# A selective-scan hybrid kernel: ScalarE's share for other stages follows a timetable of VectorE's units, and a turn gets two rooms for its column sums

## The chip, the cores and the metric

The kernel runs on one core of a Trainium2 chip. The metric is device time in microseconds (us). Three runs of the kernel before took 6051.08, 6039.0 and 6030.13 us; the median is 6039.0 us.

## The reference, cut to what matters

Four layers run on x of shape 4 x 96 x 64 x 64, image by image. Layer 0 is a selective scan over four directions k; layers 1 to 3 (an inverted-bottleneck convolution, a Fourier mixing layer with a small quantised feed-forward, a linear attention with another) need only matmuls and elementwise work. The scan is what must be seen:

```python
xs = jnp.stack([xf, xt, jnp.flip(xf, -1), jnp.flip(xt, -1)], axis=1)   # rows, columns, both reversed
def step(hst, inp):
    ut, dt_, bt, ct = inp
    dA = jnp.exp(dt_[..., None] * A[None])
    hst = hst * dA + (dt_ * ut)[..., None] * bt[:, :, None, :]
    y = jnp.einsum('bkdn,bkn->bkd', hst, ct)
    return (hst, y)
...
y = y0 + y1 + y2 + y3      # y1 and y3 come back from column order to row order
```

There are 192 channels d, 16 states n, 4096 positions, 4 directions and 4 images.

## The kernel before, in words

**Units and slots.** A unit of the scan is a tile of 128 rows (32 channels x 4 states) and 1024 positions. There are 4 images x 4 directions x 4 pieces of 1024 x 24 tiles = 1536 units. `scans` (L1234) is a Python loop over slots, one unit a slot, which writes the order of the instructions of every engine's queue by hand. A unit takes these steps:

- POOL multiplies the input by B (`inputs`, L1278, the instruction is L1280), two slots ahead, into one of 8 buffers `scan_w`.
- ScalarE makes the decay exp(delta A) (`decays`, L1282, L1287), one slot ahead, into one of two pairs of PSUM banks `ps_da`. Just ahead of it stands `keep` (L1309, L1315), which copies the last state of the unit before.
- VectorE runs the scan (`states`, L1297, L1303). The multiplication by C (`product`, L1318) follows on VectorE at once, or on POOL two slots later. `share` (L1289) chooses, so that a planned lead of the two engines over each other stays small; it uses planned times of 2.35 us for a scan and 1.2 or 2.37 us for a product.
- TensorE sums the 4 states of a channel into `ps_y` (`sums`, L1331, L1341), two units at a time, three slots later. ScalarE copies a finished `ps_y` to `yt` (`sums_out`, L1350, L1355), and SyncE stores it.

With two pairs of banks, the decay of slot s+1 can start when VectorE has left unit s-1, and it has to be done before VectorE has left unit s. Whatever stands between two decays in ScalarE's queue uses up that time.

**The other stages** stand in the same queues, beside the scan. `plan` (L1225) lists them as stages, each a set of generators that yield (engine, planned us) before an instruction, or `wait(n)` for n slots: fronts (input convolution and scan inputs of the next image), weights, turns, conv, spectral, layer_2, layer_3. At the end of each slot `advance` (L1467) issues steps of the current stage while its engine still has room (`fits`, L1454: at least half of the step's planned time). A TensorE result is used by ScalarE in the same slot only while little TensorE work has been planned in it. The room is refilled at the end of each slot by fixed amounts with a cap (`SHARE`, L59; L1404): 2.4 us up to 2.8 for ScalarE, 3.0 up to 3.2 for TensorE, 1.5 up to 2.0 for VectorE.

**A turn** (`turn`, L646) brings the sums of the two column directions back to row order and adds the row direction and the skip term. It works on three thirds of 64 channels. A third loads the two column directions into the tile `ya`, 1 MB each (L657), waits 10 slots, goes through 8 chunks (small loads L666 and L667, matmuls L672 and L674, an eviction L678, a store), and waits 2 slots. The turns of images 0 and 1 are stages of their own; those of images 2 and 3 run beside layer_3 of the image before. `big` (L198) has two buffers in all while the scans run.

**After the last unit** (image 3's convolution, spectral and last layers) no scan remains to run beside.

Of the kernel before, what the change touches and what calls it, by code (L numbers as in the profile page):

```python
# [46 lines left out]
SCAN_US, PRODUCT_US = 2.35, (1.2, 2.37)  # L47
# [8 lines left out]
WORK = {"weights": 47.0, "turn": 79.2, "front": 417.0, "conv": 447.0,  # L56
        "spectral": 111.2, "layer_2": 231.0, "product": 1.2, "layer_3": 153.6, "layer_3_turn": 232.8}
RATE = 6.0
SHARE = {"pe": (3.0, 3.2), "act": (2.4, 2.8), "dve": (1.5, 2.0)}  # L59
NQ, NG, NPAIR = 4, HID // 32, H // 2  # L60


# [35 lines left out]
def hybrid_kernel(ctx: ExitStack, tc: tile.TileContext, a: dict):  # L98


    pe, ac, dv = ((lambda us, banks=0, ind=False, e=e: (e, us, banks, ind)) for e in ("pe", "act", "dve"))
    wait = lambda n: ("wait", n, 0, False)
    nc = tc.nc
    mm = nc.tensor.matmul
    act = nc.scalar.activation
# [3 lines left out]
    pool = lambda name, bufs=1, **kw: ctx.enter_context(tc.tile_pool(name=name, bufs=bufs, **kw))  # L109
# [10 lines left out]
    def turns(of):  # L120
        of.append(of.pop(0))
        return of[-1]
# [33 lines left out]
    def const(name, rows=slice(0, 128)):  # L156
        return cst[rows, CS[name]]
# [40 lines left out]
    def big(name):  # L198
        if last_room and turns(thirds) == "last":
            return last_room[0].tile([128, 6144], F32, name=name, tag="big", bufs=1)  # L200
        return bp.tile([128, 6144], F32, name=name, tag="big", bufs=2)
# [4 lines left out]
    spare = []  # L206
# [44 lines left out]
    def split(t):  # L251
        return t.rearrange("p (a b) -> p a b", a=RPC)
# [393 lines left out]
    def turn(b):  # L646


        im = b % 2
        early = b == B - 1  # L650
        while scanned[b] < (2 if early else 3) * NCH:
            yield wait(1)
        t = big("ya")
        for r in (2, 0, 1) if early else (0, 1, 2):
            lo = 64 * r
            for at, k in ((0, 1), (64, 3)):
                load(t[at : at + 64, :L].rearrange("p (c l) -> p c l", c=NCH),  # L657
                     d_y[k][im][:, lo : lo + 64, :].rearrange("c p l -> p c l"))

            rows = not (early and r == 2)  # L660
            held = slice(0 if rows else 64, 128)

            def fetch(c):
                u = t[:, L + c % 4 * CH : L + c % 4 * CH + CH]
                if rows:
                    load(u[:64], d_y[0][im][c, lo : lo + 64])  # L666
                load(u[64:], d_skip[b][c, lo : lo + 64])  # L667
                return u

            def added(p, of):  # L670
                c, u = of
                mm(split(p[:64]), lhsT=const("two")[:, :64],  # L672
                   rhs=t[:, :L].rearrange("p (w h) -> p h w", h=H)[:, c * RPC : (c + 1) * RPC, :], start=True, stop=False)
                mm(p[:64], lhsT=skips[held, r], rhs=u[held], start=False, stop=True)  # L674

            def stored(p, of):
                s = tmp("yrow")[:64]
                nc.scalar.copy(s, p[:64])  # L678
                later(d_yt[im][of[0]][lo : lo + 64], s)

            chunks = ahead(1, fetch, range(NCH))

            ready = (lambda n: scanned[b] >= 2 * NCH + min(n + 2, NCH)) if early and rows else (lambda n: True)
            yield wait(10)
            yield from in_turn(chunks, pe(2.7, 1), added, ac(0.6), stored, ready=ready)
            yield wait(2)

    def scan_outputs(b, done):

# [544 lines left out]
    def scans(stages):  # L1234
# [13 lines left out]
        units = []  # L1248
# [33 lines left out]
        def decays(x, last):  # L1282
            if last is not None:
                keep(last)
            av = (x["step"]["k"] * NI + x["i"]) * NJ + x["j"]
            x["da"] = decay_banks()
            act(x["da"], x["step"]["d"][x["i"]], AF.Exp, scale=aneg[:, av : av + 1])  # L1287

        def share(x):  # L1289

            on_vector, on_pool = PRODUCT_US
            lead = ahead_by[0] + SCAN_US - on_pool
            x["pool"] = abs(lead - on_pool) < abs(lead + on_vector)
            lead += -on_pool if x["pool"] else on_vector
            ahead_by[0] = max(-AHEAD, min(lead, AHEAD))

        def states(x):  # L1297
            step, u = x["step"], x["u"]
            share(x)
            order = slice(None, None, -1) if step["k"] >= 2 else slice(None)  # L1300
            x["h"] = x["w"] if x["pool"] else x["da"]
            start = 0.0 if step["n"] == 0 else steps[x["number"] - 1]["last"][:, u : u + 1]
            nc.vector.tensor_tensor_scan(  # L1303
                x["h"][:, order], x["da"][:, order], x["w"][:, order], start, ALU.mult, ALU.add
            )
            if not x["pool"]:
                product(x, nc.vector)
# [23 lines left out]
        def sums(group):  # L1331
            step, first, last = group[0]["step"], group[0]["j"] == 0, group[0]["j"] == NJ - 1
            if first:
                step["y"] = bank("y")
            y = step["y"]

            made = None
            for m in (1, 0):
                for e in (1, 0):
                    q = 2 * e + m  # L1340
                    done = mm(y[32 * q : 32 * q + 32], lhsT=const("stack"), rhs=group[m]["w"][:, e * CH : e * CH + CH],  # L1341
                              start=first, stop=last)
                    if made is None:
                        made = group[0]["made"]
                        tc.add_manual_dep(done.ins, made.ins.name, mybir.DependencyInfo(
                            mybir.DependencyClass.Sync, mybir.DependencyReason.DATA), reason="sums")
            if last:
                summed.append((group, y))

        def sums_out():  # L1350
            while summed:
                group, y = summed.pop(0)
                step = group[0]["step"]
                yt = sp.tile([128, CH], F32, name="yt", bufs=1)
                nc.scalar.copy(yt, y)  # L1355
                which = group[0]["pass"]
                for e in (0, 1):
                    to = d_y[step["k"]][step["b"] % 2][2 * step["c"] + e]
                    later(to[64 * which : 64 * which + 64], yt[64 * e : 64 * e + 64],
                          (lambda b=step["b"]: through(b)) if which == len(PASSES) - 1 and e == 1 else None)  # L1360
# [9 lines left out]
        inputs(units[0])  # L1370
        inputs(units[1])
        decays(units[0], None)
        for slot in range(len(units) + 6):
            clock[0] = slot
            x = units[slot] if slot < len(units) else None
            if x is not None:
                if x["u"] == 0:


                    last = len(units) - NST * PC  # L1380
                    if slot < last:
                        rate = max(RATE, sum(s.work for s in stages if s not in behind) / (last - slot))
                    else:
                        rate = sum(s.work for s in stages) / (len(units) - slot)
                for name, i in OWN.get(x["u"], ()):
                    fetch(x["step"], name, i)
                if x["number"] + 1 < len(steps) and x["u"] in LOADS:
                    if x["u"] == 14:
                        need(steps[x["number"] + 1])
                    for name, i in LOADS[x["u"]]:  # L1390
                        fetch(steps[x["number"] + 1], name, i)
            flush()
            if slot + 1 < len(units):
                decays(units[slot + 1], units[slot - 1] if slot > 0 else None)
            sums_out()
            if slot + 2 < len(units):
                inputs(units[slot + 2])
            if 2 <= slot < len(units) + 2 and units[slot - 2]["pool"]:
                product(units[slot - 2], nc.gpsimd)
            if x is not None:  # L1400
                states(x)
            for group in due.get(slot, ()):
                sums(group)
            for e, (us, most) in SHARE.items():  # L1404
                room[e] = min(room[e] + us, most)
            tensor[0] = 0.0
            held_banks[0] -= freed[0]
            freed[0] = 0
            owed = min(owed + rate, 8.0)
            while owed > 0.0:  # L1410
                did = advance(stages)
                if did is None:
                    break
                owed -= did
                ahead_by[0] += beside[0]
                beside[0] = 0.0
        flush()


    clock, tensor = [-1], [0.0]  # L1420
    beside, ahead_by = [0.0], [0.0]
    room = {e: most for e, (_, most) in SHARE.items()}

    class Stage:

# [237 lines left out]
```

## Time and profile before

| what | value |
|---|---|
| median of three runs | 6039.0 us (6030.13 to 6051.08) |
| the profiled execution's own time | 6029.4 us |
| its span | 6027.6 us |
| before the first scan (to 88 us) | VectorE busy 17.55 us |
| the 1536 slots (88 to 5548 us) | VectorE busy 5100.19 us, POOL 5142.11, ScalarE 3632.20, TensorE 4064.35 |
| after the last scan (5548 us on) | 479.60 us, of which TensorE busy 443.55 us |
| scans on VectorE; products on VectorE and on POOL | 1536; 860 and 676 |
| granted TensorE clock over the span | 0.857 |

How to read the views: the groups give for each line the number of instructions, the engine's busy time, the mean length, and the engine's idle time just before them with what ended it. The waits give who waited for whom, in total us, times and longest us. In a timeline the idle time before an instruction stands at its end, in brackets. A wait for several semaphores is put down to the last of them. In the parts on slots, slot s begins where the s-th scan instruction of VectorE starts.

### The profile page before, as it was taken

How to read it: one execution, taken by the hardware profiler on the slowest of the kernel's cores; microseconds unless marked ns; L12 is line 12 of the kernel's file. 1: busy time of each engine (PE TensorE's matmuls, PEld its weight loads, DVE VectorE, ACT ScalarE, POOL GpSimd, SP SyncE). 2: the span in 40 equal slices, each digit the busy share in tenths (PEclk: the TensorE clock that was granted, in tenths of full speed). 3: DMA queues.
4: the chain of work that ended last, by engine and by line, in shares of the span. 5: the costliest groups of instructions: out<-in, count | busy, mean ns of one | idle time of the engine just before them, and what ended most of it. 6: DMA issues, size and time to landing. Idle time of an engine off the chain costs nothing. (4 is left out here: it accounts for less than half of the span.)

```text
span 6027.6 us, 78329 instructions
## 1 busy us (share of the span) xinstructions
PE 4564.8 (76%) x27668; PEld 1682.2 (28%) x27668; DVE 5280.0 (88%) x3583; ACT 3856.1 (64%) x6056; POOL 5154.5 (86%) x2219
## 2 busy tenths in 40 slices
PE   6743867755898776686568888768888877779998
PEld 2100212211222642121012246211222642112284
DVE  4999898899999899989999999999999999897045
ACT  4853776764665677877556657777666677665335
POOL 4987898999999999989999999999999999897000
PEclk9855978877999888797689989878999888789999
DMA  5654575667754654466776446557754664674101
GB/s 182 229 177 152 195 227 183 219 211 232 216 161 148 200 194 154 159 196 205 229 238 186 164 159 217 166 175 224 220 173 155 199 199 144 184 239 146 48 16 38
DMA packets 425084, 1078.44 MB, mean 179 GB/s; under 512 B 79378, under 2 KB 81268, under 8 KB 423540
## 3 DMA queue, kind: packets, MB, share of 16 engines
q1 hardware_dynamic: 424692, 1073.44, 56.0%
q8 instruction: 219, 3.59, 0.3%
q14 instruction: 173, 1.42, 0.1%
HBM read 857.02 MB, written 220.66 MB: 179 GB/s over the span
## 5 line engine op out<-in xcount | busy, mean ns | idle before, releaser
L1280 POOL TENSOR_TENSOR scan_w<-scan_g,scan_B 128x1024 f32<-128x1024 f32 x1536 | 3606.5, 2376 | 242.0 <-PE ps_y L1341 112.3
L1287 ACT ACTIVATE ps_da<-scan_d,aneg 128x1024 f32<-128x1024 f32 x1536 | 1714.4, 1116 | 324.3 <-DVE scan_w L1318 176.1
L1318 POOL TENSOR_TENSOR scan_w<-scan_w,scan_C 128x1024 f32<-128x1024 f32 x676 | 1605.4, 2375 | 153.3 <-ACT state L1315 102.4
L1303 DVE TENSOR_TENSOR_SCAN ps_da<-ps_da,state,scan_w 128x1024 f32<-128x1024 f32 x633 | 1483.0, 2343 | 103.8 <-ACT ps_da L1287 92.5
L1341 PE MATMUL ps_y<-scan_w,cst 128*32 128x512 f32 x6144 | 1003.0, 730 | 590.8 <-POOL scan_w L1318 297.8
L1303 DVE TENSOR_TENSOR_SCAN scan_w<-ps_da,state,scan_w 128x1024 f32<-128x1024 f32 x519 | 1214.2, 2341 | 32.9 <-ACT ps_da L1287 30.7
L1318 DVE TENSOR_TENSOR scan_w<-ps_da,scan_C 128x1024 f32<-128x1024 f32 x860 | 1053.1, 1225 | 71.7 <-DMA scan_C<-bc 6.4
L1303 DVE TENSOR_TENSOR_SCAN ps_da<-ps_da,scan_w 128x1024 f32<-128x1024 f32 x227 | 518.4, 2284 | 58.3 <-ACT ps_da L1287 51.1
L1341 PEld LDWEIGHTS ps_y<-scan_w,cst 128*32 128x32 f32 x6144 | 147.2, 117 | 1221.5 <-POOL scan_w L1318 505.1
L1315 ACT COPY state<-ps_da 128x1 f32<-128x1 f32 x654 | 104.1, 159 | 488.4 <-DVE scan_w L1318 486.5
L829 PE MATMUL ps_mm<-h,wd 128*32 128x512 f32 x3144 | 363.5, 593 | 7.0 <-ACT r L169 7.0
L1303 DVE TENSOR_TENSOR_SCAN scan_w<-ps_da,scan_w 128x1024 f32<-128x1024 f32 x157 | 357.8, 2279 | 9.5 <-ACT ps_da L1287 6.9
L567 PE MATMUL ps_mm<-xp,taps 128*128 128x512 f32 x576 | 285.9, 639 | 51.6 <-ACT xp L547 22.2
L806 PE MATMUL ps_mm<-wd,w 128*32 128x512 f32 x1944 | 243.1, 613 | 17.9 <-ACT h L810 8.7
L618 PE MATMUL ps_mm<-xd,dtw 128*128 128x512 f32 x256 | 165.4, 737 | 70.8 <-ACT z L640 43.8
L1315 ACT COPY state<-scan_w 128x1 f32<-128x1 f32 x498 | 93.2, 187 | 192.0 <-DVE scan_w L1303 191.6
L627 ACT ACTIVATE z<-ps_mm 128x512 f32<-128x512 f32 x192 | 114.4, 596 | 148.3 <-PE ps_mm L622 76.5
L633 DVE SCALAR_TENSOR_TENSOR ps_mm<-ps_mm,z 128x512 f32<-128x512 f32 x192 | 131.3, 684 | 87.7 <-ACT z L631 82.6
L888 PE MATMUL ps_mm<-r,cst 128*128 128x512 f32 x220 | 149.4, 768 | 62.4 <-ACT r L885 13.8
L672 PE MATMUL ps_mm<-ya,cst 128*64 128x512 f32 x192 | 183.2, 1043 | 9.1 <-ACT acc L912 8.6
L810 ACT ACTIVATE h<-ps_mm 128x512 f32<-128x512 f32 x258 | 150.6, 596 | 53.8 <-PE ps_mm L806 50.9
L829 PEld LDWEIGHTS ps_mm<-h,wd 128*32 128x32 f32 x3144 | 110.6, 109 | 239.8 <-issue 207.3
(360 smaller groups left out, 6536.9 us busy)
## 6 DMA issues: line engine op xcount, KB each, us to landing
scan_g<-du SPq DMA_DIRECT2D x384, 512.0 KB, 5.0
scan_d<-delta SPq DMA_DIRECT2D x384, 512.0 KB, 5.9
scan_B<-bc SPq DMA_DIRECT2D x256, 512.0 KB, 5.3
scan_C<-bc SPq DMA_DIRECT2D x256, 512.0 KB, 5.2
y<-yt SPq DMA_DIRECT2D x384, 128.0 KB, 2.7
du<-g SPq DMA_DIRECT2D x128, 256.0 KB, 3.0
delta<-z SPq DMA_DIRECT2D x128, 256.0 KB, 2.8
tab<-in_etab SPq DMA_DIRECT2D x112, 256.0 KB, 4.0
```

The costliest lines, as they stand in the source:

```text
L567: mm(p, lhsT=taps[:, t, 0:128], rhs=window(t, c + e), start=t == 0, stop=t == 8)
L618: mm(p, lhsT=dtw[:, o + 2 * third, 0:128], rhs=xd, start=True, stop=True)
L672: mm(split(p[:64]), lhsT=const("two")[:, :64], rhs=t[:, :L].rearrange("p (w h) -> p h w", h=H)[:, c * RPC : (c + 1) * RPC, :], start=True, ...
L806: mm(p[32 * n : 32 * n + 32], lhsT=w1[:, 32 * g : 32 * g + 32], rhs=xin[:, n : n + 15 : 2, 1 : W + 1], start=True, stop=True)
L810: act(h[:, :, 1 : W + 1], split(p), AF.Relu)
L829: mm(p[32 * n : 32 * n + 32], lhsT=held["wd"][:, groups[i], o, dx, :], rhs=here[i][:, :, dx : dx + W], start=dx == 0, stop=dx == 2)
L1280: nc.gpsimd.tensor_mul(x["w"], x["step"]["g"][x["i"]], x["step"]["B"][x["j"]])
L1287: act(x["da"], x["step"]["d"][x["i"]], AF.Exp, scale=aneg[:, av : av + 1])
L1303: nc.vector.tensor_tensor_scan(x["h"][:, order], x["da"][:, order], x["w"][:, order], start, ALU.mult, ALU.add)
L1315: nc.scalar.copy(step["last"][:, u : u + 1], x["h"][:, end : end + 1])
L1318: x["made"] = engine.tensor_mul(x["w"], x["h"], x["step"]["C"][x["j"]])
L1341: done = mm(y[32 * q : 32 * q + 32], lhsT=const("stack"), rhs=group[m]["w"][:, e * CH : e * CH + CH], start=first, stop=last)
```

## The change

The number of instructions on each engine, and the numbers of products on VectorE (860) and on POOL (676), are the same in both kernels; the order differs.

- ScalarE leaves `SHARE`. At the end of slot s its room grows by `spare`, the planned time of VectorE's unit s (2.35 us, or 3.55 us with the product on VectorE) plus VectorE's other work of the slot before (`took`), less 1.3 us for the decay. The cap is `spare` plus the planned time of unit s+1, less 1.35 us. A copy to `yt` takes 0.6 us from the room.
- For the timetable the engine of the next unit's product has to be known: `share` is called one slot earlier, before the slot's other work has been issued.
- A turn has two tiles, `ya` and `yb`. The first third's columns are loaded at the start, the second third's 8 slots later; 2 slots after that its chunks begin. The loads of the third after are issued when a third's chunks have ended, and the next third begins 2 slots later. `wait(2)` stands once at the end, no longer after each third.

```diff
-SHARE = {"pe": (3.0, 3.2), "act": (2.4, 2.8), "dve": (1.5, 2.0)}
+SHARE = {"pe": (3.0, 3.2), "dve": (1.5, 2.0)}
+DECAY_US, BEFORE_US, YT_US = 1.3, 1.35, 0.6
...
-        t = big("ya")
-        for r in (2, 0, 1) if early else (0, 1, 2):
-            lo = 64 * r
+        order = (2, 0, 1) if early else (0, 1, 2)
+        places = [big("ya"), big("yb")]
+
+        def columns(n):
+            t, lo = places[n % 2], 64 * order[n]
             for at, k in ((0, 1), (64, 3)):
                 load(t[at : at + 64, :L].rearrange("p (c l) -> p c l", c=NCH),
                      d_y[k][im][:, lo : lo + 64, :].rearrange("c p l -> p c l"))
 
+        columns(0)
+        for n, r in enumerate(order):
+            t, lo = places[n % 2], 64 * r
...
-            yield wait(10)
+            if n == 0:
+                yield wait(8)
+            if n + 1 < len(order):
+                columns(n + 1)
+            yield wait(2)
             yield from in_turn(chunks, pe(2.7, 1), added, ac(0.6), stored, ready=ready)
-            yield wait(2)
+        yield wait(2)
...
         def states(x):
             step, u = x["step"], x["u"]
-            share(x)
...
                 nc.scalar.copy(yt, y)
+                room["act"] -= YT_US
...
         decays(units[0], None)
+        share(units[0])
...
+            if slot + 1 < len(units):
+                share(units[slot + 1])
             for e, (us, most) in SHARE.items():
                 room[e] = min(room[e] + us, most)
+            on_vector = lambda n: SCAN_US + (0.0 if units[min(n, len(units) - 1)]["pool"] else PRODUCT_US[0])
+            spare = on_vector(slot) + took[0] - DECAY_US
+            room["act"] = min(room["act"] + spare, spare + on_vector(slot + 1) - BEFORE_US)
+            took[0] = 0.0
...
                 ahead_by[0] += beside[0]
+                took[0] += beside[0]
                 beside[0] = 0.0
...
-    room = {e: most for e, (_, most) in SHARE.items()}
+    room = {e: most for e, (_, most) in SHARE.items()} | {"act": 2.8}
+    took = [0.0]
```

## The prediction

> **What bounds the kernel now.** I read the busy times first, then the groups of the two scan engines, the waits, a timeline of one stall, and the stretches of the stages.
>
> ```profile
> PE 4564.8 (76%) x27668; PEld 1682.2 (28%) x27668; DVE 5280.0 (88%) x3583; ACT 3856.1 (64%) x6056; POOL 5154.5 (86%) x2219
> ...
> L1280 POOL TENSOR_TENSOR scan_w<-scan_g,scan_B 128x1024 f32<-128x1024 f32 x1536 | 3606.5, 2376 | 242.0 <-PE ps_y L1341 112.3
> L1287 ACT ACTIVATE ps_da<-scan_d,aneg 128x1024 f32<-128x1024 f32 x1536 | 1714.4, 1116 | 324.3 <-DVE scan_w L1318 176.1
> ...
> L1303 DVE TENSOR_TENSOR_SCAN ps_da<-ps_da,state,scan_w 128x1024 f32<-128x1024 f32 x633 | 1483.0, 2343 | 103.8 <-ACT ps_da L1287 92.5
> ```
>
> VectorE and POOL carry the scan and are about equally full. In the 5460 us of the slots POOL is busy 5142 us, VectorE 5100 us; so no more than about 318 us is to be had there, and only where both engines gain.
>
> ```profile
> DVE ps_da L1303 <- ACT ps_da L1287: 143.6, 114, 5.4
> ...
> DVE scan_w L1303 <- ACT ps_da L1287: 37.7, 54, 3.8
> ```
>
> These are VectorE's waits for a late decay: 181.3 us in 168 places, half of its idle time in the slots. The other engine's counterpart:
>
> ```profile
> POOL scan_w L1280 <- PE ps_y L1341: 112.3, 67, 5.8
> POOL scan_w L1318 <- ACT state L1315: 102.4, 78, 6.6
> ```
>
> The second line is the state copy, which stands ahead of a decay in ScalarE's queue and is late with it. Next a stall in a spectral stage, first ScalarE, then VectorE:
>
> ```profile
> 2003.13 0.87 ACT L1055 ACTIVATE f<-ps_mm 128x384 f32<-128x384 f32 x1 [2.11 <-PE ps_mm L1047]
> 2006.95 0.83 ACT L1055 ACTIVATE f<-ps_mm 128x384 f32<-128x384 f32 x1 [2.95 <-PE ps_mm L1047]
> 2007.58 0.21 ACT L1315 COPY state<-scan_w 128x1 f32<-128x1 f32 x1
> 2007.63 1.13 ACT L1287 ACTIVATE ps_da<-scan_d,aneg 128x1024 f32<-128x1024 f32 x1
> ```
> ```profile
> 2008.86 2.36 DVE L1303 TENSOR_TENSOR_SCAN ps_da<-ps_da,state,scan_w 128x1024 f32<-128x1024 f32 x1 [4.86 <-ACT ps_da L1287]
> ```
>
> Three evictions stand between two decays. Their own work is 2.5 us, but two of them wait 5.1 us for TensorE, and VectorE loses 4.86 us. So the stall has two ingredients: too much work in a slot, and work asked for sooner than TensorE delivers. Attributing each of the 168 stalls to what ScalarE did between the two decays, 120.8 us fall where its waits for TensorE cover more than half of the stall, 60.4 us on the rest, mostly plain work.
>
> ```profile
> 1342.00:1499.00 157.00, 101.12 (x302) 17.70 (x302) 153.32 (x85) 79.06 (x132) 152.93 (x67) 0.76 0.77 233
> 1499.00:1933.00 434.00, 374.80 (x2248) 112.05 (x2248) 418.07 (x255) 267.96 (x411) 426.73 (x184) 0.93 0.57 183
> 1933.00:2180.00 247.00, 193.75 (x2845) 149.91 (x2846) 223.05 (x142) 160.41 (x243) 225.82 (x98) 0.90 0.58 190
> ```
>
> These rows are a turn, a conv and a spectral stage (after the length: TensorE, weight loads, VectorE, ScalarE, POOL busy; clock; DMA share; GB/s). Turn and conv leave POOL hardly any idle time; spectral leaves 21.2 us.
>
> **What stays.** After the last scan both orders hold the same instructions (304 on VectorE), so the 480 us there and the 88 us ahead of the first scan stay. In the slots the same work is only moved. One unit's steps keep their order and engines (860 and 676 products). `share` one slot earlier no longer sees VectorE's other work of that slot, but the lead is summed on, so it is corrected a slot later: 0, with a bound of one unneeded wait a front, some 2 us each way.
>
> **ScalarE's timetable.** Old room: 2.4 us a slot. New: 2.35 - 1.3 = 1.05 us after a unit with its product on POOL, 2.25 us after one on VectorE, plus VectorE's other work. At 676 and 860 units that is 1.72 us on average, plus 633 us of other work / 1536 = 0.41. I laid the slots of both orders side by side and summed ScalarE's work between decays at the trace's mean durations: 1.38 us becomes 1.22 us beside POOL-product units, 1.23 us becomes 1.36 us beside the others. The sum over slots of what exceeds the allowance is the overrun. Against the measured stalls, by stage:
>
> - spectral (three, 204 slots): stalls 45.3 us; overrun 53.4 to 28.5 us
> - fronts (366): 59.0; 110.1 to 116.3
> - layer_2 (191): 20.9; 58.1 to 51.7
> - layer_3, alone or beside a turn (159): 33.5; 52.5 to 40.2
> - conv (455): 22.6; 33.0 to 44.5
>
> Scaled by its overrun, each changes by -21.1, +3.3, -2.3, -7.9, +7.9 us: together **-20 us**. The largest term can be looked at directly. In the six passages of L1055 the old order has 24 slots of three evictions, and 41.2 us of stalls follow them; the new one has 19, and stretches a passage from 7 slots to 8 or 9, so TensorE gets more time for each. Spectral grows from 66 slots to 75 or 76. Those slots come from the turns (51 to 33). Bounds for spectral: 0, if the waits for TensorE only move, and -45. When the stall is gone POOL is late next; its idle time in these three stretches is 42 us, so 21 us fit.
>
> **POOL's state copies.** Grouping the 676 POOL products by ScalarE's work in their slot, waits average 0.25 us at 2 to 3 us of work and 0.51 us at 3 to 4 us. Those groups shrink from 154 to 114 and from 40 to 26 units; with all groups 102.4 becomes 94.3 us. I take **-8 us** in full, since POOL is the fuller engine; 0 if it is the same time as VectorE's stalls.
>
> **The turn.** It issues the same DMAs. The Trainium skill ("Trainium Kernel Development and Optimization", Best Practices) advises double buffering to overlap DMA with compute. Taken as a price it would give the eight later column loads of the four turns back: 8 x 12.3 us = 98 us. The trace denies it: nobody waits for L657, since the scans fill those slots (POOL busy 152.93 of 157 us). So the second room itself is worth 0; its cover is the scan. What it moves is SyncE's queue: each 2 MB of columns now stands ahead of the next third's small loads, which follow 2 slots, 6.2 us, later.
>
> ```profile
> DMA to landing us min/median/max: 7.8/12.3/16.8
> ```
>
> That is L657, a 1 MB load. "SBUF — State Buffer" (The DMA setup-cost knee) gives 2 us plus bytes at 436 GB/s: an estimated 6.8 us for the 2 MB, so 0.6 us left to wait, 5 us over eight thirds. By the row 6.1 us are left, 49 us over eight. Behind it TensorE's sums are queued, then POOL's buffers. But in the old turns TensorE already waits 62.6 us for the skip loads at L674, and VectorE loses 0.4 us by it. I take **+4 us**, bounds 0 and 49. The turn's DMA rate also rises: 16 MB packed from 157 into 104 us, beside the scans' loads, puts 233 GB/s to about 285, under the 305 that the trace reaches in 20 us stretches.
>
> **The sum.** -20 - 8 + 4 = -24 us. The profiled execution's own 6029.4 us would become 6005. It lies 9.6 us below the median of 6039.0, which I use for the forecast: **6015 us**.
>
> **Rivals.**
>
> *The waits move with the work.* Two thirds of the stalls are waits for TensorE, which no timetable of VectorE sees. For it: the long stalls all show them. Against it: the triple evictions thin out. If only the 60.4 us of plain overrun scale: -20 x 60.4 / 181.3 = -7, POOL 0, the turn +4: 6036 us.
>
> *Bursts (slower).* The new cap lets room grow to 4.45 us and more. Slots with over 4 us of side work rise from 15, all Silu pairs, to 35, mostly in the fronts, with six to nine instructions of two streams in a row. The 15 cost 21.4 us, 1.4 us each; the one over 5 us beside a VectorE product cost 2.3 us. At 2.3 us twenty more cost 46; with spectral's -21 and +4 that is +29: 6068 us. Against it: the cap grants them only when the next unit is long. It decides from 1.2 us each, where they eat the 24.
>
> *The change does nothing visible*, all terms near 0, is the first rival's neighbour and counted with it.
>
> **Chances.** Forecast 0.57 (its own range 5986 to 6030), waits move 0.23, bursts or the turn's full price 0.20. About 0.3%, 18 us, is what a measurement of this kernel can tell from no change. The forecast gives 0.48 to faster and 0.09 to within; the second 0.03, 0.19 and 0.01; the third 0.03 to within and 0.17 to slower. So faster 0.51, within 0.31, slower 0.18. The range: down to spectral's bound (-45 - 8 = -53, 5986), up to where most of the burst case begins, 6056.
>
> **What would show it.** Right: VectorE's waits for L1287 near 161 us, those after L1055 near 22, POOL's for L1315 near 94; 75 spectral slots at under 3.45 us instead of 3.51 to 3.63 us; turns of about 104 us with VectorE never idle. Wrong: waits for L1287 near or above 181 us with fronts above 62, stalls behind slots of two streams, or POOL waiting in the turns. A cost in the balance of POOL and VectorE that no slot sum shows would also break it.

## The result, and the profile after

The changed kernel takes 6070.36 us (median of 5 runs, 6067.37 to 6087.95), against 6039.0 us before: ratio 1.0064, 95% interval 1.005 to 1.0077. The median rose by 31 us where the forecast said 24 us less. The profiled execution took 6069.84 us (before: 6029.4), so the traces below show the rise as 40 us.

First the busy times and the groups that answer to those shown of before:

```profile
PE 4594.1 (76%) x27668; PEld 1708.8 (28%) x27668; DVE 5269.5 (87%) x3583; ACT 3860.4 (64%) x6056; POOL 5151.5 (85%) x2219
...
L1290 POOL TENSOR_TENSOR scan_w<-scan_g,scan_B 128x1024 f32<-128x1024 f32 x1536 | 3604.7, 2375 | 286.1 <-PE ps_y L1350 132.4
L1297 ACT ACTIVATE ps_da<-scan_d,aneg 128x1024 f32<-128x1024 f32 x1536 | 1714.3, 1116 | 318.9 <-DVE scan_w L1327 203.9
...
L1312 DVE TENSOR_TENSOR_SCAN ps_da<-ps_da,state,scan_w 128x1024 f32<-128x1024 f32 x641 | 1503.1, 2345 | 158.5 <-ACT ps_da L1297 143.3
```

The instructions of the scan did not get longer. VectorE's scans wait more for their decays, and POOL more for TensorE's sums. The waits say how much (L1312 is the scan, L1297 the decay, L1324 the state copy in the new numbering), first VectorE's, then POOL's:

```profile
DVE ps_da L1312 <- ACT ps_da L1297: 189.1, 132, 12.7
...
DVE scan_w L1312 <- ACT ps_da L1297: 60.5, 38, 12.7
```
```profile
POOL scan_w L1290 <- PE ps_y L1350: 132.4, 59, 14.3
...
POOL scan_w L1327 <- ACT state L1324: 108.7, 92, 8.9
```

Late decays cost 249.6 us instead of 181.3, and the longest wait went from 5.4 to 12.7 us: a new kind of stall. The stretches say where. These are the turn of image 0, the conv and the spectral stage after it, the same stages as shown of before:

```profile
1328.00:1451.00 123.00, 87.02 (x232) 15.64 (x232) 98.64 (x54) 53.72 (x92) 99.36 (x44) 0.82 0.83 242
1451.00:1885.00 434.00, 373.19 (x2252) 111.40 (x2248) 418.71 (x255) 271.46 (x422) 428.35 (x185) 0.94 0.55 178
1885.00:2158.00 273.00, 216.28 (x2886) 164.02 (x2886) 252.69 (x158) 172.97 (x254) 257.14 (x112) 0.84 0.58 191
```

The turn lasts 123 us; its 32 slots would take 100 us at the old turn's 3.12 us each. VectorE and POOL, hardly idle in the old one, both lose about 24 us. One stall of that turn in four timelines: SyncE, TensorE, ScalarE, VectorE.

```profile
1330.97 0.56 SPq L1275 DMA_DIRECT2D scan_C<-bc  x1
1331.62 1.30 SPq L660 DMA_DIRECT2D yb<-y  x2
1332.97 0.67 SPq L1275 DMA_DIRECT2D scan_g<-du  x1
1333.69 0.61 SPq L1275 DMA_DIRECT2D scan_B<-bc  x1
1334.34 0.60 SPq L1275 DMA_DIRECT2D scan_g<-du  x1
1335.04 0.55 SPq L1275 DMA_DIRECT2D scan_d<-delta  x1
1335.63 0.60 SPq L672 DMA_DIRECT2D ya<-y  x1
1336.28 0.59 SPq L673 DMA_DIRECT2D ya<-skip  x1
```
```profile
1332.86 1.96 PE L678 MATMUL ps_mm<-ya,cst 128*64 128x512 f32 x2
1352.09 1.94 PE L680 MATMUL ps_mm<-ya,skips 128*64 128x512 f32 x2 [17.27 <-DMA ya<-skip]
```
```profile
1337.60 1.12 ACT L1297 ACTIVATE ps_da<-scan_d,aneg 128x1024 f32<-128x1024 f32 x1
1354.07 0.58 ACT L684 COPY yrow<-ps_mm 64x512 f32<-64x512 f32 x1 [15.35 <-PE ps_mm L680]
1354.55 0.15 ACT L1324 COPY state<-ps_da 128x1 f32<-128x1 f32 x1
1354.73 1.12 ACT L1297 ACTIVATE ps_da<-scan_d,aneg 128x1024 f32<-128x1024 f32 x1
```
```profile
1355.94 2.36 DVE L1312 TENSOR_TENSOR_SCAN ps_da<-ps_da,state,scan_w 128x1024 f32<-128x1024 f32 x1 [12.73 <-ACT ps_da L1297]
```

Read it from the top. SyncE issues the next third's columns (L660, 2 MB), four loads of the scan (512 KB each), and only then the small loads of the first chunk. The skip load, issued at 1336.28, is there at 1352; L680 waits 17.27 us for it. The chunk's eviction L684 stands ahead of the next decay in ScalarE's queue and waits 15.35 us with it; the decay follows, and VectorE has lost 12.73 us. POOL, behind the sums that are queued on TensorE after L680, loses 13.12 us at the same place. The skip loads' landing times, in the kernel before and in the changed one:

```profile
DMA to landing us min/median/max: 2.5/4.0/6.8
```
```profile
DMA to landing us min/median/max: 2.5/4.1/15.7
```

The median did not move; the load in the wrong place did. Late decays by stage, worked out from the timeline of VectorE (us, before to after): the two turns alone 0.0 to 41.9; layer_3 beside a turn 28.5 to 59.9; together +73. Spectral 45.3 to 37.5, fronts 59.0 to 56.1, layer_2 20.8 to 22.5, layer_3 alone 4.9 to 4.8, conv 22.6 to 26.9: together -5. VectorE's other idle time in the slots fell from 178.5 to 164.2 us, all of it and more in the fronts (88.0 to 62.2), and its busy time by 10 us. 68.3 - 14.3 - 10.4 = 44 us more in the slots; 477 instead of 480 us after the last scan.

### The profile page after: what moved, and what is told of

It reads as the page before. It is cut to its first block, busy times and chain, and to the rows that moved or that the text cites. A ratio compares the mean times of both kernels' runs of the same rounds, so it can differ in the third digit from the quotient of the medians.

```text
span 6068.1 us, 78364 instructions
## 1 busy us (share of the span) xinstructions
PE 4594.1 (76%) x27668; PEld 1708.8 (28%) x27668; DVE 5269.5 (87%) x3583; ACT 3860.4 (64%) x6056; POOL 5151.5 (85%) x2219
## 5 line engine op out<-in xcount | busy, mean ns | idle before, releaser
L1297 ACT ACTIVATE ps_da<-scan_d,aneg 128x1024 f32<-128x1024 f32 x1536 | 1714.3, 1116 | 318.9 <-DVE scan_w L1327 203.9
L1327 POOL TENSOR_TENSOR scan_w<-scan_w,scan_C 128x1024 f32<-128x1024 f32 x676 | 1604.2, 2373 | 155.5 <-ACT state L1324 108.7
L1312 DVE TENSOR_TENSOR_SCAN ps_da<-ps_da,state,scan_w 128x1024 f32<-128x1024 f32 x641 | 1503.1, 2345 | 158.5 <-ACT ps_da L1297 143.3
L1350 PE MATMUL ps_y<-scan_w,cst 128*32 128x512 f32 x6144 | 990.5, 722 | 482.3 <-POOL scan_w L1327 264.8
L1312 DVE TENSOR_TENSOR_SCAN scan_w<-ps_da,state,scan_w 128x1024 f32<-128x1024 f32 x511 | 1194.0, 2340 | 47.1 <-ACT ps_da L1297 34.4
L1312 DVE TENSOR_TENSOR_SCAN ps_da<-ps_da,scan_w 128x1024 f32<-128x1024 f32 x219 | 500.5, 2285 | 59.1 <-ACT ps_da L1297 45.7
L1324 ACT COPY state<-ps_da 128x1 f32<-128x1 f32 x651 | 102.8, 158 | 525.9 <-DVE scan_w L1327 524.9
L1312 DVE TENSOR_TENSOR_SCAN scan_w<-ps_da,scan_w 128x1024 f32<-128x1024 f32 x165 | 375.2, 2278 | 28.4 <-ACT ps_da L1297 26.1
L1324 ACT COPY state<-scan_w 128x1 f32<-128x1 f32 x501 | 93.3, 186 | 167.3 <-DVE scan_w L1312 166.8
L1012 PE MATMUL ps_mm<-wa,xp 128*64 128x96 f32 x1728 | 132.6, 312 | 54.9 <-DVE d L1021 31.6
L684 ACT COPY yrow<-ps_mm 64x512 f32<-64x512 f32 x96 | 55.6, 580 | 181.5 <-PE ps_mm L680 174.0
```

The source lines that it names most:

```text
L1312: nc.vector.tensor_tensor_scan(x["h"][:, order], x["da"][:, order], x["w"][:, order], start, ALU.mult, ALU.add)
L1324: nc.scalar.copy(step["last"][:, u : u + 1], x["h"][:, end : end + 1])
L1327: x["made"] = engine.tensor_mul(x["w"], x["h"], x["step"]["C"][x["j"]])
```

## The experiments

Two theories stood first. **Burst**: the small loads wait behind the columns, and that costs the 73 us in the turns; the timetable saves about 30 us elsewhere. **Timetable**: ScalarE's new timetable makes the stalls, and the second room is harmless.

All results on one page. "Slots" is the time from the first scan to the end of the last in the profiled execution, "end" what follows, "turns" the late decays in the four turns (alone and beside layer_3), "all" in all slots. The ratio is to the kernel before on the same chip, where it took 6037 to 6042 us (median).

| kernel | median us | ratio, 95% interval | slots | end | turns | all |
|---|---|---|---|---|---|---|
| before | 6039.0 | | 5460 | 480 | 28.5 | 181 |
| changed | 6070.36 | 1.0064, 1.005 to 1.0077 | 5504 | 477 | 101.8 | 250 |
| e1 timetable only | 6103.79 | 1.0106, 1.0093 to 1.012 | 5432 | 582 | 27.6 | 185 |
| e2 two rooms only | 6086.01 | 1.0076, 1.0062 to 1.0089 | 5541 | 459 | 99.7 | 253 |
| e3 six slots | 6087.83 | 1.0072, 1.0056 to 1.0088 | 5452 | 546 | 28.6 | 202 |
| e4 columns in pieces | 6035.57 | 0.999, 0.9981 to 0.9999 | 5470 | 479 | 63.6 | 217 |
| e5 small loads first | 6036.44 | 0.9997, 0.9985 to 1.0009 | 5474 | 480 | 66.1 | 219 |
| e6 pieces and first | 6025.61 | 0.9981, 0.9971 to 0.999 | 5461 | 480 | 55.6 | 209 |
| e7 e6 without timetable | 6041.61 | 1.0007, 0.9995 to 1.0019 | 5498 | 459 | 59.0 | 212 |
| e8 e6 with fixed share | 6048.88 | 1.0014, 1.0005 to 1.0024 | 5472 | 489 | 33.0 | 190 |
| e9 columns on other queue | 6054.84 | 1.003, 1.0019 to 1.0042 | 5495 | 480 | 76.4 | 238 |
| e10 e6, two chunks ahead | 6016.17 | 0.997, 0.996 to 0.9981 | 5451 | 481 | 48.6 | 202 |
| e11 e7, share early | 6035.96 | 0.9995, 0.9983 to 1.0007 | 5491 | 463 | 60.7 | 217 |
| e12 e6, twiddle at 1.1 | 6020.11 | 0.9966, 0.9954 to 0.9977 | 5457 | 482 | 55.6 | 201 |

**One part at a time.** e1 is the changed kernel with the old `turn`:

```diff
-        places = [big("ya"), big("yb")]
+        t = big("ya")
...
+            yield wait(10)
             yield from in_turn(chunks, pe(2.7, 1), added, ac(0.6), stored, ready=ready)
+            yield wait(2)
```

> The changed kernel with the old turn (one room, 12 waiting slots a third). Burst theory: the new turn's small loads wait behind 2 MB of columns and cost about 73 us of late decays in the four turns, the timetable saves about 34 us elsewhere. Here the turns have no stalls again (VectorE's waits for decays about 176 us instead of 235), but without the shorter turns the timetable leaves 228 more TensorE instructions of the last conv behind the last scan; at the old tail's pace (about 0.27 us each) that is +60 us. So about 6039 - 34 + 60 = 6065 us, with the scans ending about 34 us earlier than in the kernel before. Rival, the timetable itself makes the stalls: the scans end no earlier than in the changed kernel, 6100 us or more.

6103.79 us. The total is where the rival had it, but not for its reason: the turns are back at the 28 us of before and the slots take 28 us less than before, as the burst theory has it. But 102 us are added after the last scan, not 60. 468 more matmuls start there than before (4702 against 4234, twice the expected 228) and 48 more ScalarE instructions, nearly all of the last conv, in a stretch where no scan runs beside them. Part of the 28 us is such work moved out of the slots. So the timetable alone costs 61 us, and the shorter turns are what pays for its longer spectral stages.

e2 is the kernel before with the new `turn`.

> The kernel before with the new turn alone. Burst theory: +73 us of stalls in the turns, while 90 fewer TensorE instructions are left behind the last scan (-24 us): about 6088 us. Rival, the timetable makes the stalls and the two rooms are harmless: 6039 - 24 = 6015 us, and no decay waits in the turns.

6086.01 us, 99.7 us of late decays in the turns without any timetable. The timetable theory falls; the turn makes the stalls.

**What in the turn.** e3 leaves more time between the columns and the chunks:

```diff
                 columns(n + 1)
-            yield wait(2)
+            yield wait(6)
```

> The changed kernel with 6 instead of 2 slots between the columns' loads and the third's chunks. Burst theory: 19 us are more than the 14 to 16 us that the small loads needed, so the turns' stalls of 73 us go; 180 more TensorE instructions fall behind the last scan (+49 us): about 6046 us, scans ending some 70 us earlier than in the changed kernel. Rival, the timetable makes the stalls: 6070 + 49 = 6119 us.

The stalls in the turns are back at the level of before (28.6 us against 28.5), which is the burst theory's main point. The total missed by 42 us: the 4 slots a third cost 69 us after the last scan instead of 49, and layer_2, now elsewhere in the scan, has 44 us of late decays instead of 23.

e4, e5, e6 and e10 leave the order of all compute instructions as it is; in their traces the sequences of ScalarE, VectorE and POOL are those of the changed kernel, instruction by instruction. e4 loads the next third's columns in 8 pieces, one behind the small loads of each chunk (the new argument of `columns` is left out here):

```diff
                 load(u[64:], d_skip[b][c, lo : lo + 64])
+                if n + 1 < len(order):
+                    columns(n + 1, slice(c, c + 1))
                 return u
...
-            if n + 1 < len(order):
-                columns(n + 1)
```

e5 issues the first two chunks' small loads ahead of the columns:

```diff
-            chunks = ahead(1, fetch, range(NCH))
...
+            while not ready(0):
+                yield wait(1)
+            first = [fetch(0), fetch(1)]
+            chunks = ahead(1, lambda c: first[c] if c < 2 else fetch(c), range(NCH))
             if n + 1 < len(order):
                 columns(n + 1)
             yield wait(2)
```

> The changed kernel, its order of all compute instructions untouched, but the next third's columns are loaded in 8 pieces of 2 x 128 KB, each behind the small loads of a chunk. Burst theory: the small loads have at most 256 KB of columns ahead of them, the turns' stalls go, about 6070 - 73 = 5997 us, under the kernel before. Rival, the DMA engines' total rate or ScalarE's new timetable makes the stalls: the same bytes in the same slots, so within 10 us of 6070.

> The changed kernel, compute order untouched; the small loads of a third's first two chunks are issued ahead of the next third's 2 MB of columns instead of 2 slots behind them. Same bytes, same slots. Place-in-the-queue theory: the 10 to 17 us waits at the first chunk go; chunks 2 and 3 still stand behind the columns, with some 3 us left to wait. Of the 73 us that the turns cost about 50 come back: about 6020 us. Rival, the DMA engines' rate is what is short: within 10 us of 6070.

6035.57 and 6036.44 us: 35 and 34 us come back from the order of the loads alone, about half of the 73 that the turns had lost, where 73 and 50 were expected. The late decays in the turns fall by 38 and 36 us. The other expectation, 6070 us for the same bytes in the same slots, is out. e6 does both:

> The changed kernel with both: columns in 8 pieces behind a chunk's small loads, and the first two chunks' small loads 2 slots ahead of their matmuls. In the pieces run decay waits of 64 us were left in the four turns, at first chunks whose small loads had no lead. Lead theory: these fall to the 28 us of the kernel before, so 6036 - 35 = about 6001 us. Rival, the shorter turn is too dense for TensorE and ScalarE whatever the loads do: 6030 to 6036 us.

6025.61 us, faster than both kernels, but 25 us short of the lead theory's number: 55.6 us of late decays stay in the turns. ScalarE's waits for the turn's matmul, in the changed kernel and in e6:

```profile
ACT yrow L684 <- PE ps_mm L680: 174.0, 76, 16.6
```
```profile
ACT yrow L686 <- PE ps_mm L682: 123.3, 71, 6.0
```

The long ones are gone, many short ones remain. e10 asks whether more lead removes them:

```diff
-            ready = (lambda n: scanned[b] >= 2 * NCH + min(n + 2, NCH)) if early and rows else (lambda n: True)
+            ready = (lambda n: scanned[b] >= 2 * NCH + min(n + 3, NCH)) if early and rows else (lambda n: True)
...
-            first = [fetch(0), fetch(1)]
-            chunks = ahead(1, lambda c: first[c] if c < 2 else fetch(c), range(NCH))
+            first = [fetch(0), fetch(1), fetch(2)]
+            chunks = ahead(2, lambda c: first[c] if c < 3 else fetch(c), range(NCH))
```

> The run with pieces and first loads, its small loads two chunks ahead of the matmuls instead of one. There 56 us of decay waits are left in the four turns, against 28 in the kernel before. Lead theory: another chunk of lead (3 us) takes some 15 us off: about 6011 us. Rival, the denser turn itself: unchanged, 6025 us within 5.

6016.17 us, 9 us less than e6 (the intervals overlap), with 48.6 us of late decays in the turns. Lead helps a little. It is the lowest median here, 0.3% under the kernel before. From the changed kernel to e10 the order of the loads alone is worth 54 us, and takes 53 of the 73 us of late decays out of the turns.

**Queue or engines.** e9 is the changed kernel with the columns issued at the same place, from ScalarE's own DMA queue:

```diff
-                load(t[at : at + 64, :L].rearrange("p (c l) -> p c l", c=NCH),
+                nc.scalar.dma_start(t[at : at + 64, :L].rearrange("p (c l) -> p c l", c=NCH),
```

> The changed kernel, the columns' loads at their old place in time, but issued from ScalarE's own DMA queue instead of SyncE's, so the small loads do not stand behind them in one queue. Queue-order theory: the waits at the first chunks go, as far as in the run with the small loads first: about 6036 us, plus 24 issues on ScalarE of about 0.6 us each, at most 15 us: 6036 to 6050. Rival, sharing of the 16 DMA engines: the 2 MB take the bandwidth all the same, 6065 us or more, with the small loads landing after 10 us or more at the first chunks.

6054.84 us, between the two expectations, and the turns keep 76.4 of the 101.8 us. SyncE's timeline shows why:

```profile
1327.42 0.56 SPq L1275 DMA_DIRECT2D scan_C<-bc  x1
1328.03 0.66 SPq L1275 DMA_DIRECT2D scan_g<-du  x1
1328.74 0.59 SPq L1275 DMA_DIRECT2D scan_B<-bc  x1
1329.38 0.60 SPq L1275 DMA_DIRECT2D scan_g<-du  x1
1330.08 0.55 SPq L1275 DMA_DIRECT2D scan_d<-delta  x1
1330.73 0.55 SPq L672 DMA_DIRECT2D ya<-y  x1
1338.80 0.48 SPq L673 DMA_DIRECT2D ya<-skip  x1
```

The columns are on another queue, and still the skip load is issued 8 us after its neighbour: SyncE's next issue came when the scan load of 1327.42 had landed, after 11.4 us (the median of these loads in the changed kernel is 5.2). The bytes ahead are on the same DMA engines. This agrees with the Trainium skill, "DMA: Bandwidth & Descriptors" (Issuing engines are not separate DMA queues): another issuing engine saves issue time, not transfer time. Earlier issue or smaller pieces took 36 to 38 us of late decays out of the turns (e4, e5), another queue 25.

Why SyncE stood just there can be read from the traces too. The loads and stores of the program signal eight semaphores in turn, and each waits until the one eight ahead of it has landed. Among some 2510 issues of SyncE with a known landing, none came before that, in the kernel before as in the changed one. The landing that SyncE waited for in e9 is that of the load eight ahead in the order of the changed kernel, which the first timeline of the turn shows: the two columns hold two of the eight places whichever queue issues them. In the changed kernel SyncE's next issue after 1336.28 is at 1340.67, when the first of the columns has landed. In all it stood 98 us for such landings, against 34 us in the kernel before and 63 us in e6. So a bulk load delays the small ones twice: by its bytes, and by its place.

**The timetable's worth.** e7 is e6 without the timetable, e8 has instead the timetable's mean as a fixed amount (`"act": (2.13, 2.8)`), e11 is e7 with `share` one slot earlier.

> The kernel before (ScalarE's room 2.4 us a slot) with the turn of the run with pieces and first loads. Theory that the timetable saves about 25 us in the slots: those 25 are missing, while 90 fewer TensorE instructions behind the last scan give 20 back: 6001 + 25 - 20 = about 6006 us. Rival, the timetable saves nothing and the earlier end of the scans with it was work pushed behind the last scan: about 5980 us.

> The same, with ScalarE's room at a fixed 2.13 us a slot (cap 2.8), which is the mean that the timetable grants, and no timetable. Amount theory: what helps is that less ScalarE work is asked for in a slot, wherever it stands, so this equals the run with timetable, pieces and first loads, about 6001 us, within 8. Timetable theory: the place in long and short units matters, so it is 15 us or more above that run, about 6020.

> The run without the timetable, with the product's engine chosen one slot earlier as the timetable needs it. If that step is free, as the prediction had it: 6041.6 us within 8. Rival, the older information costs: VectorE and POOL wait more for each other, 6055 us or more. Second rival, the earlier choice is itself what the timetable's runs gain by: about 6025.

e7: 6041.61 us. The timetable is worth 16 us with a sound turn: 37 us in the slots, less 21 us by what e7 does not leave after the last scan. (The expected number was built on 6001 us for e6, 25 us too low; against e6 it was 5 us, and 16 were measured.) e8: 6048.88 us, 23 us above e6, 11 us of it in the slots and 9 after them, so the mean amount alone does not do it. The timetable also has a higher cap (4.45 us and more, against 2.8), which was not varied alone, so place and cap are not told apart. e11: 6035.96 us, not to be told from e7; no cost of the earlier choice shows. Of the 37 us in the slots 24 are VectorE's idle time apart from late decays, 11 its busy time and 3 late decays. The idle time fell in the fronts, from 81 to 60 us, and mostly in a row of VectorE that is no scan, softplus waiting for ScalarE's logarithm in the fronts, first in e7, then in e6:

```profile
DVE ps_mm L633 <- ACT z L631: 80.0, 20, 32.5
```
```profile
DVE ps_mm L634 <- ACT z L632: 50.5, 9, 33.0
```

Four waits of each, 43 and 44 us, lie ahead of the first scan; the rest falls from 37 to 7 us. e8 has 78.6 us in this row, like e7. Late decays are nearly the same in both (212 and 209 us). Why the logarithm comes earlier under the timetable was not followed up.

e12 plans the spectral product of L1047 at its measured 1.1 us (4 matmuls of 275 ns) instead of 0.7:

> The run with pieces and first loads, where the spectral product of L1047 is planned at 1.1 us of TensorE (4 matmuls of 0.275 us) instead of 0.7, so that no slot gets more of them than TensorE delivers. If the stalls left in spectral (33 us) are work asked for sooner than TensorE can deliver: they fall by 10 to 15 us, about 6012 us. Rival, they are TensorE waiting for its tables from DMA or for the sums ahead of it: no change, 6025 us within 5.

6020.11 us, 5 us under e6 (the intervals overlap). ScalarE's waits for that product (L1059 in both), e6 and e12:

```profile
ACT f L1067 <- PE ps_mm L1059: 43.6, 27, 4.6
```
```profile
ACT f L1067 <- PE ps_mm L1059: 27.7, 29, 2.3
```

Late decays in spectral fall from 32.9 to 25.5 us, some 7 us where 10 to 15 were expected. So a part of them is work asked for sooner than TensorE delivers, and the timetable, which knows only VectorE, leaves it. e12's total cannot be told from e10's either; the two together were not run.

## Why the prediction was wrong

- **What stays** was right: 477 us after the last scan (480), 87 us ahead of the first (88), the same products. `share` one slot earlier shows no cost (e11).
- **The turn, +4 us with bounds 0 and 49**, is the step that turned the sign: it cost 73 us of late decays. Four pieces of it failed.
  - The lead of 2 slots, put at 6.2 us, was 4.0 us (1331.62 to 1335.63), since SyncE stood until 1330.97 for a buffer of the scan.
  - The 2 MB were priced alone, and by the landing of one half: both halves took 14.1 us. Four scan loads, another 2 MB, were issued between, and the skip load landed 20 us after the columns' issue instead of 12.3.
  - The queue that I named behind the wait, TensorE's sums and then POOL's buffers, was there (POOL's 13.12 us). The way that I left out was ScalarE's own queue: eviction, state copy, decay.
  - The old waits for the skip loads were taken as a cover. They are none; the lines below show why.
- **The timetable, -20 us by late decays**, was right in sign and wrong in place. With a sound turn the timetable was worth 16 us (e6 against e7); that this is near 20 is luck, since only 3 of the 37 us that it saves in the slots are late decays. With the old turn it costs 61 us (e1). Outside the turns late decays fell by 5 us, spectral by 7.8 instead of 21.1. Scaling a stall by the overrun of planned work assumes that the stall is work; in two thirds of the old late decays, by their time, ScalarE's waits for TensorE covered more than half, as the first rival said, and those for spectral's product L1047 stayed (48.6 us before, 45.0 after). The fronts' gain of 26 us sat in VectorE's waits for L631, a row of 82.6 us in the waits of before that the prediction passed over because no scan stands in it.
- **POOL's state copies, -8 us**: 102.4 became 108.7 us; with the turns in it this says little of the timetable alone.
- **The rivals.** The slower case had the right sign and the wrong cause: late decays in the fronts, where the bursts stand, fell from 59.0 to 56.1 us. The turn's full price was on the page, as a bound of 49 us, with too small a chance; even that bound was short of 73.

The cover, in two lines of the kernel before:

```profile
1344.10 1.97 PE L674 MATMUL ps_mm<-ya,skips 128*64 128x512 f32 x2 [7.25 <-DMA ya<-skip]
1347.05 0.57 ACT L678 COPY yrow<-ps_mm 64x512 f32<-64x512 f32 x1
```

TensorE waited 7 to 9 us for a skip load four times there, but ScalarE never more than 2.8 us for the result: here the matmul is 7 us late, and the eviction comes later still and waits for nothing. The 17.27 us in the changed kernel outlasted that slack, and ScalarE stood 15.35 us. The 0.4 us that I took for VectorE's loss stand in the views at L672, the other matmul, and such a row doesn't follow a wait through ScalarE's queue. Followed through it, 7.5 us of late decays in the kernel before have an L678 ahead of them, and 81.3 us in the changed one have an L684.

The fit of the Trainium skill's "SBUF — State Buffer" (The DMA setup-cost knee), an estimated 6.8 us for the 2 MB, was further off than the row of 12.3 us. The section's 436 GB/s is the rate of all 16 ports, and it counts a load into 64 partitions, as each half of the columns is, no faster than one into 32. So the fit was not made for these loads.

What stays open: why e6 and e10 keep 20 to 27 us more late decays in the turns than the kernel before. The denser turn alone is not the answer, since e8 has the same turn and 33.0 us. e7 and e8 differ only in ScalarE's fixed amount, 2.4 and 2.13 us a slot, and have 59.0 and 33.0 us, so the amount of ScalarE's side work bears on it; how, no run shows.

## What to carry to other kernels

Before moving a bulk load ahead of small ones, list everything that the issuing queue puts between the bulk load and the first use of a small one, in bytes and in loads that may be out at once, and find which in-order queue waits for that use. Here 54 of the changed kernel's 6070 us came back by the order of the loads alone, with all compute in the same order. Read a wait on the engine whose queue carries the critical work: a late result is harmless only while its reader comes later still. And in a kernel whose side work fills slots of a fixed number, a slower stage is paid for after the last slot (e1: 102 us), so a change is to be judged with its counterpart.

## What the runs showed of the hardware that was not expected

- Moving the columns to a second DMA queue left 76 of 102 us of the late decays in the turns, and SyncE's next issue waited for one of its own scan loads to land (8 us between 1330.73 and 1338.80).
- No load or store of SyncE was issued before the one eight ahead of it had landed (some 2510 issues each in the kernel before and the changed one; 215 and 253 came before the one seven ahead had). The traces show this as waits for the program's eight semaphores, so it is how this program is built, and not shown to be a limit of the chip.
- Under the 2 MB, loads of 512 KB on the way took 14 to 16 us instead of a median of 5 to 6 (in the changed kernel, `scan_g` of 1332.97 landed after 14.0 us).
